# Recurrent layers: the scan's end states copied by ScalarE instead of VectorE, and the norm's power issued in two halves, one before and one after the next step's adding transfer

## The chip, the cores and the metric

The kernel runs on one core of a Trainium2 chip. The metric is the device time of one execution in microseconds (us). The engines are named as in the profile: PE is the matrix engine (PEld its weight loads), DVE is VectorE, ACT is ScalarE, POOL is GpSimd, SP issues plain transfers. Each engine works through its own instructions in the order in which the program wrote them[...].

## The reference

Four blocks follow each other on x of 4 batches x 512 positions x 512 channels, all in 32-bit floats: a cross attention (layer 0), two RWKV layers (layers 1 and 2), and a perceiver layer with an MLP (layer 3). The change touches layers 1 and 2 alone. In each of these, after the projections r, k, v, g and the decay w, a recurrence runs over the positions for every head (32 heads of 16 channels), and its output is normalised per head:

```python
def step(s, inp):
    k_l, v_l, w_l, r_l = inp
    a = k_l[..., :, None] * v_l[..., None, :]
    out = jnp.einsum('bhs,bhst->bht', r_l, faaaa * a + s)
    return a + w_l[..., None] * s, out
_, outs = jax.lax.scan(step, s0, seq)
gm = jnp.mean(y, axis=-1, keepdims=True)
gv = jnp.mean((y - gm) ** 2, axis=-1, keepdims=True)
y = ((y - gm) * jax.lax.rsqrt(gv + EPS)).reshape(B, L, C) * gn_w + gn_b
x = x + y * g @ Wo.T
```

The factor `rsqrt(gv + EPS)` is the power that the change cuts in two. The state s that one half of a sequence leaves to the other is what the copies carry. Around this stand a layer norm and the mixing of neighbouring positions before the recurrence, and a channel block (norm, two gates, three products) after it.

## The kernel before, in words

**Units and steps.** A unit is one layer, one batch and one half of the 512 positions: 16 units, numbered 0 to 15 here. Even units are first halves, odd units second halves, which start from the state that the even unit before them left. A unit has eight scan steps, 0 to 7 here. They are global steps g = 8 * unit + step, and one loop runs over g. At each g it emits, in this order: `summed(g - 1)` (four matmul groups on PE that sum the step before over the state), `begun(g + 1)`, `scan(g)`, at every fourth step `repeated` (PE writes the v rows of the coming four steps into the PSUM tile `vr`), and then whatever the generators have put down for this step in four phases, EARLY, SOON, MID and LATE. In the MID phase of steps 0 and 4, `taken` (L894) adds the sums `py` of the four steps before to `y`.

**What a step does.** `begun(g + 1)` (L833 to L844) has DVE write two products of k and v, one into the tile `kv` (two buffers, used in turn) and one into the tile `A` (a single buffer), and the state into the first column of `kv` (the copy at L839). Then POOL issues a transfer that adds `A` onto `kv` in SBUF (`added`, L584), and ACT spreads the decay into the tile `W` (L844). `scan(g)` (L862) runs the recurrence on DVE over `kv`; two more DVE products (`ry`, L867) follow, for PE. In even units a small DVE copy at L864 stands between the scan and the products; it saves the last column of `kv` as the state `S`. So one step's adding transfer has to land before DVE may write `A` for the following step, and before its own `kv` is scanned.

**What else runs in the steps.** Three generators per unit are laid over the steps by hand: each `yield` names the step, counted from the unit's own first step, and the phase in which the generator goes on. `mixes(q)` prepares unit q in the twelve or so steps before it (norm, projections, decay), `outputs(q)` normalises unit q from its step 9, that is step 1 of the following unit, and `channels(q)` does the channel block from step 19, that is step 3 of the unit after that. In a given unit, work of three other units is thus interleaved. After unit 15 the steps go on without scans until the last generators are done; this stretch, about 2,290 to 2,412 us, is called the drain here. Then layer 3 begins.

**The power.** `outputs` forms the variance on PE, adds the epsilon on DVE (L927, step 10, LATE), raises 128x64 values to the power -0.5 on POOL (L929, step 11, EARLY), and spreads the result over `rp` with four ACT copies (L933, step 12, LATE). PE multiplies `rp` out at step 13 (`pbc`), ACT copies it (L938), and DVE scales y with it (L940). On POOL's queue the power is followed, still in step 11, by the two small norm instructions of `channels` (L79 and L552) and by two adding transfers of the channel block (`x<-xr`, L584), and then, in step 12, by the adding transfer of `begun(13)`. Counted in the unit whose scan is running, the power stands in step 3 and that transfer belongs to step 5's `kv`.

**Three more names.** `td` (L735) and `o_w` (L744, L750) are ACT's work on the decay of the next unit, in the LATE phase of step 2 and the EARLY phase of step 3; they wait for PE. `o_g` (L717) is DVE's gating of g around step 6, which frees the PSUM tiles that PE's transposes `ptn` (L572) want next.

Of the kernel before, what the change touches and what calls it, by code (L numbers as in the profile page):

```python
# [11 lines left out]
ALU = mybir.AluOpType  # L12
# [18 lines left out]
def tile_xattn_rwkv_perceiver(ctx: ExitStack, tc: tile.TileContext, t: dict, out: bass.AP):  # L31
    nc = tc.nc
# [7 lines left out]
    mhalf = const.tile([P, TS // 4], F32, name="mhalf")  # L40
# [30 lines left out]
    def mm(ps, pairs):  # L71
        for i, (lhsT, rhs) in enumerate(pairs):
            nc.tensor.matmul(ps, lhsT, rhs, start=(i == 0), stop=(i == len(pairs) - 1))  # L73
# [22 lines left out]
    def psum_tile(shape, name):  # L96
        pool, tag = psum["p"]
        return pool.tile(shape, F32, tag=tag, name=name)
# [356 lines left out]
    def recurrent(lp, ep):  # L455
# [5 lines left out]
        TP = TS // 2  # L461
        EARLY, SOON, MID, LATE = range(4)
# [67 lines left out]
        def flat(a):  # L530
            return a.rearrange("p a l -> p (a l)")
# [314 lines left out]
        def place(g):  # L846
            q, j = divmod(g, G)
            return q, j // NI, j % NI

        def quarters(kv):  # L850
            return kv.rearrange("p (q f) l -> p q f l", f=2)

        def states(q):
            return st[q]["S"].rearrange("p i (q e f) -> p i e q f", e=2, f=2)

        def scan(g):

            q, e, i = place(g)
            d = st[q]
            kv = kvs.pop(g)  # L860

            nc.vector.tensor_tensor_scan(flat(kv), flat(W[g % 2]), flat(kv), 0.0, ALU.mult, ALU.add)  # L862
            if units[q][2] == 0:
                nc.vector.tensor_copy(states(q)[:, i, e], quarters(kv)[:, :, :, TP])  # L864
            for h in range(2):
                y = ys[g, h] = mp.tile([P, 4, 2, TP], F32, tag="ry", name="ry", bufs=4)
                nc.vector.tensor_tensor(  # L867
                    y,
                    kv[:, 4 * h : 4 * h + 4, None, :TP].to_broadcast([P, 4, 2, TP]),
                    d["r"][:, i].rearrange("p (o m) -> p o m", o=2)[:, None].to_broadcast([P, 4, 2, TP]),  # L870
                    ALU.mult,
                )
# [23 lines left out]
        def outputs(q):  # L896

            li, b, hf = units[q]
            n = f"L{li}_"
            c, d = small[li], st[q]  # L900
            y = d["y"]
            NQ = TS // 4
            full = [P, NI, TS]
            pm = psum_tile([P, TS], "pmean")
            mm(pm, [(gmean, y[:, i, :]) for i in range(NI)])
            mean = sp.tile([P, TS], F32, tag="mean", name="mean", bufs=1)
            nc.scalar.copy(mean, pm)
            yield 9, LATE
            nc.vector.tensor_tensor(y, y, mean[:, None, :].to_broadcast(full), ALU.subtract)
            yield 10, EARLY  # L910
            sq = mp.tile(full, F32, tag="cx", name="sq", bufs=BUFS["cx"])
            nc.scalar.activation(sq, y, AF.Square)
            yield 10, SOON
            var = psum_tile([P, NQ], "var")
            for i in range(NI):
                for a in range(4):
                    nc.tensor.matmul(
                        var[32 * a : 32 * a + 32],
                        gm32,
                        sq[:, i, NQ * a : NQ * a + NQ],  # L920
                        start=(i == 0),
                        stop=(i == NI - 1),
                        tile_position=(0, 32 * a),
                    )
            yield 10, LATE
            rstd = sp.tile([P, NQ], F32, tag="gn_rs", name="gn_rs")
            nc.vector.tensor_scalar(rstd, var, 1.0, 1e-5, ALU.mult, ALU.add)  # L927
            yield 11, EARLY
            nc.gpsimd.tensor_tensor(rstd, rstd, mhalf[:, :NQ], ALU.pow)  # L929
            yield 12, LATE  # L930
            for a in range(4):
                rs = slice(32 * a, 32 * a + 32)
                nc.scalar.copy(rp[rs, NQ * a : NQ * a + NQ], rstd[rs])  # L933
            yield 13, EARLY
            pm = psum_tile([P, TS], "pbc")
            mm(pm, [(gself, rp)])
            bc = sp.tile([P, TS], F32, tag="mean", name="bc", bufs=1)
            nc.scalar.copy(bc, pm)  # L938
            yield 13, LATE
            nc.vector.tensor_tensor(y, y, bc[:, None, :].to_broadcast(full), ALU.mult)  # L940
            yield 14, EARLY

            yg = mp.tile(full, F32, tag="cx", name="yg", bufs=BUFS["cx"])
            for i in range(NI):
                nc.scalar.activation(
                    yg[:, i].rearrange("p (m o) -> p o m", o=2),
                    y[:, i].rearrange("p (o m) -> p o m", o=2),
                    AF.Identity,
                    bias=c["gn"][:, i, 1:2],
                    scale=c["gn"][:, i, 0:1],  # L950
                )
            nc.gpsimd.tensor_tensor(yg, yg, d["g"], ALU.mult)
            yield 15, MID
            wo = wpool.tile([P, NI, C], F32, tag="w", name=n + "wo")
            for a in range(4):
                nc.sync.dma_start(
                    wo[32 * a : 32 * a + 32], t[n + "Wo"].rearrange("(h a i) n -> a h i n", a=4, i=NI)[a]
                )
            pms = []
            for lt in range(NT):  # L960
                pm = psum_tile([P, C], "pm")
                mm(pm, [(yg[:, i, lt * P : (lt + 1) * P], wo[:, i, :]) for i in range(NI)])
                pms.append(pm)
            yield 15, LATE
            for lt in range(NT):
                x = xn[b][hf * NT + lt]
                nc.vector.tensor_tensor(x, pms[lt], x, ALU.add)
# [74 lines left out]
        steps = {}  # L1042
# [6 lines left out]
        for q in range(len(units)):  # L1049
            if q > 0:  # L1050
                follow(q, (-13 if q == 1 else -11, LATE), mixes(q))
            follow(q, (9, EARLY), outputs(q))
            follow(q, (19, LATE), channels(q))
        end = G * len(units)
        with (
            tc.tile_pool(name="rm", bufs=2) as mp,
            tc.tile_pool(name="rs", bufs=2) as sp,
            tc.tile_pool(name="rpv", bufs=1, space=PSUM) as pvr,
            tc.tile_pool(name="rpy", bufs=1, space=PSUM) as pyp,
            tc.tile_pool(name="rpp", bufs=3, space=PSUM) as pp,  # L1060
        ):
            psum["p"] = pp, "p"


            W = [mp.tile([P, 8, TP + 1], F32, tag=f"W{i}", name=f"W{i}", bufs=1) for i in range(2)]
            A = mp.tile([P, 8, TP + 1], F32, tag="A", name="A", bufs=1)
            for z in (*W, A):
                nc.gpsimd.memset(z[:, :, 0:1], 0.0)
            for g in range(at[0], end + 28):
                if 0 < g <= end:  # L1070
                    summed(g - 1)
                if -1 <= g < end - 1:
                    begun(g + 1)
                if 0 <= g < end:
                    scan(g)
                if 0 < g < end - 2 and g % NI == NI - 2:
                    repeated(*place(g + 2)[:2])
                for ph in (EARLY, SOON, MID, LATE):
                    for q, gen in steps.pop((g, ph), ()):
                        at = next(gen, None)  # L1080
                        if at:
                            follow(q, at, gen)
                    if ph == MID and 0 < g <= end and g % NI == 0:
                        taken(g - 1)
# [325 lines left out]
    with (  # L1410
        tc.manual_schedule(engines={E.PE, E.DVE, E.Activation, E.Pool}),
        tc.tile_pool(name="rl", bufs=1) as lp,
        tc.tile_pool(name="rt", bufs=2) as ep,
    ):
        ahead = recurrent(lp, ep)
        layer0(ahead, ep)
        for _ in ahead:
            pass
# [66 lines left out]
```

## Time and profile before

| what | value |
|---|---|
| time, median of 3 runs | 3794.02 us (3792.13 to 3795.58) |
| the profiled execution's own time | 3798.02 us |
| its span | 3796.2 us |
| granted PE clock, mean | 0.966 |
| scans of the 16 units | about 778 to 2,290 us |
| POOL power L929 (128x64) | 16, 11.65 us each |
| DVE copy of the state L864 | 64, 0.88 us each |
| DVE copy of the state L839 | 128, 0.17 us in the middle |
| DVE products L867 | 256, 1.40 us each |
| DVE waiting for an adding transfer before A L833 | 87.8 us, 38 times |

In the profile's lines a group reads: line, engine, operation, output<-inputs, size, count, then busy time, mean ns of one, and idle time of the engine before them with what ended it. In the timeline a line gives start, duration, engine, line, operation, and in brackets how long the engine had been idle and who released it; instructions of one line that follow each other are merged into one row with a count. Where an engine waits for several things, the row names the one that came last.

### The profile page before, as it was taken

What the parts mean: (1) busy time and instruction counts of PE and PEld (TensorE: products, weight loads), DVE (VectorE), ACT (ScalarE), POOL (GpSimd) and SP (SyncE); (2) the same over time, 40 slices, a digit from 0 to 9 for tenths busy, and PEclk for the clock granted to TensorE, in tenths of its full rate; (3) what the DMA queues carried; (4) which work ended last, traced back from release to release, by engine and by line L of the source; (5) the groups of instructions that cost most, each with busy time, mean ns of one, the idle gap of its engine ahead of it and who ended that gap; (6) DMA issues with size and microseconds to landing.
All of it is one profiled execution on the core that took longest, in us unless ns stands there. A gap on an engine that the chain in (4) does not pass through costs nothing.

```text
span 3796.2 us, 52369 instructions
## 1 busy us (share of the span) xinstructions
PE 3570.5 (94%) x20544; PEld 1900.4 (50%) x20544; DVE 2759.9 (73%) x4665; ACT 1668.2 (44%) x2486; POOL 1771.0 (47%) x834
## 2 busy tenths in 40 slices
PE   9999999988899999999999977799999999999989
PEld 3333333455565666655655544444455445544446
DVE  6777777689988888888888882177866766667531
ACT  4777675533444444444444432133334434434421
POOL 4777876524544444444444443045533433344330
PEclk9999999989999999999999988899999999999999
DMA  4000000156676777777777764400022122121223
GB/s 151 24 12 23 12 9 20 40 141 141 146 171 165 170 188 177 170 173 179 163 171 167 169 156 111 111 28 19 15 76 83 56 70 95 56 73 34 95 95 122
DMA packets 188805, 386.66 MB, mean 102 GB/s; under 512 B 18128, under 2 KB 44880, under 8 KB 186512
## 3 DMA queue, kind: packets, MB, share of 16 engines
q1 hardware_dynamic: 150256, 251.72, 20.9%
q0 software_dynamic: 38304, 131.61, 18.7%
q8 instruction: 162, 2.65, 0.3%
q14 instruction: 83, 0.68, 0.1%
HBM read 247.50 MB, written 4.19 MB: 66 GB/s over the span
## 4 chain that ended last, share of the span: by engine, by line
PE 71%; DVE 13%; DMA 6%; issue 4%; POOL 3%; ACT 2%; SPq 0%; DVEq 0%; POOLq 0%; ACTq 0%
PE pm L73 9%; PE ph L73 6%; PE pv L73 6%; PE po L73 6%; DMA kv<-A 5%; PE psc L242 5%; PE pst L279 4%; PE pst L1175 4%; PE psc L1175 4%; PE pr L73 3%; PE pk L73 3%; PE po L304 3%; PE po L1241 3%; DVE ry L867 3%; DVE kv L862 2%
## 5 line engine op out<-in xcount | busy, mean ns | idle before, releaser
L1236 POOL TENSOR_TENSOR acc<-acc,aT 128x2048 f32<-128x2048 f32 x96 | 436.2, 4544 | 337.5 <-ACT aT L1231 220.0
L292 POOL TENSOR_TENSOR aT<-aT,nmT 128x1536 f32<-128x1536 f32 x124 | 428.7, 3461 | 205.5 <-ACT aT L290 182.2
L254 DVE CUSTOM_DVE_ANT_0 sc<-psc,nm 128x512 f32<-128x512 f32 x512 | 354.1, 692 | 147.2 <-PE psc L242 89.5
L1220 DVE TENSOR_TENSOR aT<-pst,mb 128x512 f32<-128x512 f32 x512 | 317.7, 683 | 166.0 <-PE pst L1175 166.0
L867 DVE TENSOR_TENSOR ry<-kv,o_r 128x1024 f32<-128x1024 f32 x256 | 347.4, 1398 | 3.5
L584 POOL DMA_DIRECT2D kv<-A x127 | 118.8, 936 | 381.4 <-DVE kv L839 378.3
L862 DVE TENSOR_TENSOR_SCAN kv<-W,kv 128x1032 f32<-128x1032 f32 x128 | 296.3, 2315 | 0.2 <-DMA kv<-A 0.2
L290 ACT COPY aT<-pst 128x512 f32<-128x512 f32 x372 | 196.5, 595 | 177.9 <-PE pst L279 177.4
L298 ACT ACTIVATE aT<-aT 128x2048 f32<-128x2048 f32 x128 | 246.7, 1929 | 5.4 <-POOL aT L292 4.6
L73 PE MATMUL ph<-nT,l_m 128*128 128x256 f32 x1024 | 238.1, 388 | 0.0
L73 PE MATMUL po<-l_m,hT 128*128 128x512 f32 x512 | 233.1, 602 | 0.0
L73 PEld LDWEIGHTS ph<-nT,l_m 128*128 128x128 f32 x1024 | 193.6, 193 | 64.1 <-issue 24.8
L833 DVE TENSOR_TENSOR A<-vr,o_k 128x1024 f32<-128x1024 f32 x128 | 155.7, 1217 | 87.9 <-DMA kv<-A 87.8
L279 PE MATMUL pst<-q,km 32*128 32x512 f32 x1024 | 206.5, 640 | 9.4 <-DVE mxs L254 5.8
L1234 POOL TENSOR_TENSOR acc<-aT 128x2048 f32<-128x2048 f32 x16 | 72.4, 4527 | 303.2 <-ACT aT L1229 303.2
L1189 DVE CUSTOM_DVE_ANT_0 sc<-psc,zeros,mx 128x512 f32<-128x512 f32 x256 | 176.6, 746 | 51.2 <-PE psc L1175 49.0
L1231 ACT ACTIVATE aT<-aT 128x2048 f32<-128x2048 f32 x64 | 122.3, 1911 | 191.8 <-DVE aT L1220 191.6
L1229 ACT ACTIVATE aT<-aT,mc 128x2048 f32<-128x2048 f32 x64 | 128.1, 2002 | 165.1 <-DVE aT L1220 158.9
L242 PE MATMUL psc<-km,q 32*128 32x512 f32 x1024 | 198.5, 651 | 0.8 <-ACT q L223 0.8
L929 POOL TENSOR_TENSOR gn_rs<-gn_rs,mhalf 128x64 f32<-128x64 f32 x16 | 186.4, 11648 | 23.1 <-DVE gn_rs L927 23.1
L881 PE MATMUL py<-ry,k 128*32 128x512 f32 x1024 | 159.6, 637 | 39.1 <-DVE ry L867 27.6
L1189 DVE CUSTOM_DVE_ANT_0 sc<-psc,nm 128x512 f32<-128x512 f32 x256 | 161.1, 686 | 39.2 <-PE psc L1175 39.2
(265 smaller groups left out, 7153.3 us busy)
## 6 DMA issues: line engine op xcount, KB each, us to landing
l_m<-in_L_W SPq DMA_DIRECT2D x64, 1024.0 KB, 5.1
kv<-A POOLq DMA_DIRECT2D x127, 516.0 KB, 7.4
L_wk<-in_L_Wk SPq DMA_DIRECT2D x16, 1024.0 KB, 8.0
L_wr<-in_L_Wr SPq DMA_DIRECT2D x16, 1024.0 KB, 7.7
L_wv<-in_L_Wv SPq DMA_DIRECT2D x16, 1024.0 KB, 5.9
L_wg<-in_L_Wg SPq DMA_DIRECT2D x16, 1024.0 KB, 8.0
L_wo<-in_L_Wo SPq DMA_DIRECT2D x64, 256.0 KB, 7.6
L_fk<-in_L_fWk SPq DMA_DIRECT2D x16, 1024.0 KB, 7.8
```

The costliest lines, as they stand in the source:

```text
L73: nc.tensor.matmul(ps, lhsT, rhs, start=(i == 0), stop=(i == len(pairs) - 1))
L242: nc.tensor.matmul(psc, d["q"][g][rs, lt * P : (lt + 1) * P], d["km"][rs, a, :], start=True, stop=True, tile_position=(32 * r, 0),)
L254: nc.vector.tensor_tensor_reduce(sc, ps[r], d["nm"][lt], 1.0, -3.0e38, ALU.add, ALU.max, mxs[:, a, lt, c : c + 1])
L279: nc.tensor.matmul(pst, d["km"][rs, a, s * P : (s + 1) * P], d["q2", a][rs, :], start=True, stop=True, tile_position=(32 * r, 0),)
L292: nc.gpsimd.tensor_tensor(w[:, n:, :], w[:, n:, :], nmT[:, None, :].to_broadcast([P, NR - n, L]), ALU.add)
L298: nc.scalar.activation(w, w, AF.Exp)
L862: nc.vector.tensor_tensor_scan(flat(kv), flat(W[g % 2]), flat(kv), 0.0, ALU.mult, ALU.add)
L867: nc.vector.tensor_tensor(y, kv[:, 4 * h : 4 * h + 4, None, :TP].to_broadcast([P, 4, 2, TP]), d["r"][:, i].rearrange("p (o m) -> p o m", o ...
L1175: nc.tensor.matmul(psc, lhsT[rs], rhs[rs], start=True, stop=True, tile_position=(32 * r, 0))
L1189: nc.vector.tensor_tensor_reduce(sc, ps[r], d["nm"][a], 1.0, mx[:, 0, lt, r : r + 1] if a else 3.0e38, ALU.add, ALU.min, mx[:, a, lt, r : ...
L1220: nc.vector.tensor_tensor(w[:, r, :], ps[r], d["mb"][:, r, :], ALU.subtract)
L1236: nc.gpsimd.tensor_tensor(d["acc", m], d["acc", m], w, ALU.add)
```

## The change

The copy of the end state leaves DVE's place behind the scan. It is put down as a small generator `kept` that runs in the SOON phase of the same step, behind that step's EARLY work, as an ACT copy. The power on 128x64 is replaced by two on 128x32: the first stands where the whole one stood (step 11, EARLY), the second in the EARLY phase of step 12, behind the adding transfer that `begun(13)` issues at the start of step 12. The step and phase in which the ACT copies to `rp` are emitted stay.

```diff
@@ -853,6 +853,10 @@
+        def kept(dst, src):
+            nc.scalar.copy(dst, src)
+            yield from ()
+
         def scan(g):
@@ -861,7 +865,7 @@
             nc.vector.tensor_tensor_scan(flat(kv), flat(W[g % 2]), flat(kv), 0.0, ALU.mult, ALU.add)
             if units[q][2] == 0:
-                nc.vector.tensor_copy(states(q)[:, i, e], quarters(kv)[:, :, :, TP])
+                steps.setdefault((g, SOON), []).append((q, kept(states(q)[:, i, e], quarters(kv)[:, :, :, TP])))
@@ -926,7 +930,9 @@
             nc.vector.tensor_scalar(rstd, var, 1.0, 1e-5, ALU.mult, ALU.add)
             yield 11, EARLY
-            nc.gpsimd.tensor_tensor(rstd, rstd, mhalf[:, :NQ], ALU.pow)
+            nc.gpsimd.tensor_tensor(rstd[:, : NQ // 2], rstd[:, : NQ // 2], mhalf[:, : NQ // 2], ALU.pow)
+            yield 12, EARLY
+            nc.gpsimd.tensor_tensor(rstd[:, NQ // 2 :], rstd[:, NQ // 2 :], mhalf[:, : NQ // 2], ALU.pow)
             yield 12, LATE
             for a in range(4):
```

## The prediction

> **What bounds the kernel now.** I read the page's busy times and its chain first, then a table of stretches, then the timelines of PE, POOL, DVE and ACT through the scans.
>
> ```profile
> PE 3570.5 (94%) x20544; PEld 1900.4 (50%) x20544; DVE 2759.9 (73%) x4665; ACT 1668.2 (44%) x2486; POOL 1771.0 (47%) x834
> PE 71%; DVE 13%; DMA 6%; issue 4%; POOL 3%; ACT 2%; SPq 0%; DVEq 0%; POOLq 0%; ACTq 0%
> 1200.00:1600.00 400.00, 376.44 (x2535) 242.32 (x2536) 355.00 (x371) 180.94 (x360) 188.86 (x123) 0.99 0.75 176
> ```
>
> The third line is a stretch of four units: PE 376 of 400 us, DVE 355, ACT 181, POOL 189, clock 0.99, the DMA engines 75% busy. In the scans PE is the bound and a unit takes 95 to 100 us; what can be won is PE's idle time, 5 to 7 us a unit. Time taken off DVE, ACT or POOL counts only where PE stops for it. So I listed every stop of PE and asked which of them leads back to the power. Around the power of unit 7, POOL first:
>
> ```profile
> 1465.00 0.85 POOL L584 DMA_DIRECT2D kv<-A  x1 [1.79 <-DVE kv L839]
> 1465.56 11.72 POOL L929 TENSOR_TENSOR gn_rs<-gn_rs,mhalf 128x64 f32<-128x64 f32 x1
> 1477.26 0.69 POOL L79 TENSOR_TENSOR rs_cx<-rs_cx,mhalf 128x2 f32<-128x2 f32 x1
> 1479.62 1.81 POOL L584 DMA_DIRECT2D x<-xr  x2
> 1480.79 1.53 POOL L584 DMA_DIRECT2D kv<-A  x1
> ```
>
> and DVE and PE beside it:
>
> ```profile
> 1472.23 0.16 DVE L78 TENSOR_SCALAR rs_cx<-ln_mv 128x2 f32<-128x2 f32 x1
> 1477.28 0.20 DVE L839 COPY kv<-S 128x8 f32<-128x8 f32 x1
> 1484.99 0.69 DVE L894 TENSOR_TENSOR y<-py,y 128x512 f32<-128x512 f32 x1 [2.84 <-PE py L881]
> 1490.96 1.22 DVE L833 TENSOR_TENSOR A<-vr,o_k 128x1024 f32<-128x1024 f32 x1 [3.01 <-DMA kv<-A]
> 1502.97 1.14 PE L814 MATMUL vr<-o_v,vsel 32*128 32x512 f32 x8 [0.45 <-DVE A L833]
> 1516.56 1.12 PE L572 MATMUL ptn<-ident,z 128*128 128x128 f32 x4 [2.92 <-DVE o_g L717]
> ```
>
> DVE has all that the transfer needs at 1477.5, but POOL is behind the power, two small norm instructions and two other adding transfers, and issues it at 1480.79. It lands at 1490.93, DVE writes the next A 3.01 late, the transfer after that lands late too, and PE stops for DVE's A before vr (0.45) and for o_g before ptn (2.92). Over units 1 to 13 the stops before vr that follow a power are 1.98, 3.83, 0.26, 1.50, 1.24, 0.45, 2.50, 2.44, 0.19 and 2.57 (units 1, 2, 3, 4, 5, 7, 9, 10, 11, 13), 16.96 us in all. Before ptn, six units (3, 4, 5, 7, 11, 12) stop for 2.8 to 3.0.
>
> **The power in halves.** A 128x32 power is not in the trace. From the rows 11.72 (64 columns) and 0.69 (2 columns) it is 0.178 a column, so 0.69 + 30 x 0.178 = 6.0; below, half of 11.72 is 5.9; above, the whole 11.72, which 0.69 for two columns excludes. I take 6.0. In unit 7 the first half ends at 1471.6; the norm's 0.69 waits for DVE until 1472.4, its second instruction (0.2 where nothing holds it, 1.6 at most) and the two transfers (1.8) are out by 1475.3 to 1476.7. The transfer is issued when DVE allows it, at 1477.28 + 0.46 (the distance in the step before, 1464.54 to 1465.00) = 1477.7: 3.1 us earlier. The same sum gives 4.6 in unit 1, about 6 in 2 and 13, 4.5 in 5 and 9. The second half lies at 1478.3 to 1484.3. Behind it on POOL is the adding transfer of mix_g, which DVE frees only at 1487, and ACT's copies to rp come at 1492: 3 and 8 us of cover. Without that cover the next transfer would be late by the part that sticks out, 6.0 at most.
>
> What PE gets: 16.96 less the 0.16 by which unit 2's stop (3.83) exceeds the wait before A that can vanish (3.67), so 16.8. The 2.9 before ptn falls only to what units have in which DVE is earlier: stops before ptn plus the following one before py are 1.7, 2.0, 1.2, 0.8 and 1.3 in units 6, 8, 9, 10, 13, mean 1.4. So 1.5 in each of six units, 9.0.
>
> A rule speaks against this part. The Trainium skill ("SBUF — State Buffer", Who interferes with whom) says that a DVE instruction with two SBUF inputs is blocked by a POOL instruction that reads SBUF, for all of its length. Then the second half would hold step 4's ry from 1479.8 to 1484.3; it would end at 1486.6, y (L894) would follow 1.6 later than now, and 15 units would pay up to 24 us. But ry at 1466.95 took 2.36 for its pair in the middle of the whole power, as without it. For the power the row decides: nothing.
>
> **The copies.** Rows and rule agree on the 128x1024 products of POOL:
>
> ```profile
> 1371.33 0.17 DVE L864 COPY S<-kv 128x8 f32<-128x8 f32 x1
> 1407.24 3.26 POOL L772 TENSOR_TENSOR ruk<-ruk,o_k 128x1024 f32<-128x1024 f32 x1
> 1408.37 2.17 DVE L864 COPY S<-kv 128x8 f32<-128x8 f32 x1
> 1435.31 4.33 DVE L867 TENSOR_TENSOR ry<-kv,o_r 128x1024 f32<-128x1024 f32 x2
> ```
>
> The copy is 0.17 (0.08 until the next begins) or, in 23 of 64, about 2.1, held to the end of a POOL product. Read alone, that is 23 x 2.1 = 48 us to win on DVE. But ry also has two SBUF inputs, and in odd units, which have no copy, the ry at the same places is held instead (4.33 for a pair of 2.35). The hold goes to ry; DVE keeps 64 x 0.09 = 6 us, off PE's path: nothing. On ACT a 128x8 copy isn't in the trace; 128x4 and 32x64 take 0.20 and 0.24: 0.2 each, 13 us, under ACT's 56% idle.
>
> The new wait costs more. The next-but-one kv uses the same buffer, so DVE may not write it before ACT has copied, and ACT copies only behind its EARLY work. In step 3 that is o_w, which waits for PE (unit 6):
>
> ```profile
> 1376.75 1.22 DVE L833 TENSOR_TENSOR kv<-vr,o_k 128x1024 f32<-128x1024 f32 x1
> 1379.35 1.06 ACT L750 ACTIVATE o_w<-o_w 128x1024 f32<-128x1024 f32 x1
> 1389.26 0.69 DVE L894 TENSOR_TENSOR y<-py,y 128x512 f32<-128x512 f32 x1 [2.35 <-PE py L881]
> ```
>
> The kv product moves from 1376.75 to 1380.7, A from 1380.93 to 1381.8, and the transfer goes out at 1383.6: 1.9 earlier than now, not 3.0. In units 4, 8, 10 and 12 the same sum leaves 2.0, 1.3, 2.5 and 1.4, still about what their stops need. Everything queued on DVE behind (A, the scan, ry) is late by 1.0, 1.1, 3.1, 1.8 and 4.1 in units 4, 6, 8, 10, 12, against 2.42, 2.35, 4.51, 3.18 and 5.51 that DVE waits for py before y anyway: covered. In step 1 the copy is behind mix_r and costs DVE 0.7, in step 7 ACT waits 0.9 for the scan, with xr behind it; both vanish in later waits. I add nothing.
>
> **The end.** In unit 15's scan the power of unit 14 (2250.90) holds the transfer until 2265.90; DVE has it ready at 2260.4, and all that follows waits for it: 5.5 less, I take 5.4. In the drain it turns round:
>
> ```profile
> 2330.34 0.16 DVE L78 TENSOR_SCALAR rs_cx<-ln_mv 128x2 f32<-128x2 f32 x1
> 2332.76 1.52 ACT L561 ACTIVATE z<-x,ln_mv,rs_cx 128x512 f32<-128x512 f32 x2
> 2332.93 1.83 POOL L584 DMA_DIRECT2D x<-xr  x2 [0.28 <-issue]
> 2341.90 1.22 PE L73 MATMUL pm<-L_wo,yg 128*128 128x512 f32 x1 [5.80 <-POOL yg L952]
> ```
>
> The whole power started at 2321.13 while POOL had nothing else. The second half stands behind the norm that waits for DVE until 2330.5 and behind two transfers, so it runs from about 2333.4 to 2339.2; ACT's rp ends 1.0 later, and z, queued behind it, starts at 2340.0 instead of 2332.76. The chain goes on through yg to PE without slack: +7.2.
>
> **Sum.** -16.8 - 9.0 - 5.4 + 7.2 = -24.0. The profiled execution: span 3796.2 and 1.8 around it, 3798.0, so 3774.0. The median shown is 4.0 under that execution, so I forecast 3770.
>
> **Rivals.**
> - *The transfers land no earlier.* They share DMA engines that are 70 to 75% busy, and took 7.4 in the middle but 12.3 in unit 9. If half of the body's 25.8 goes there or into the next stop: -11, 3783. For it: the landing times vary. Against: the queue only gets the same transfers sooner. Chance 0.2.
> - *More than summed.* Stops before ptn vanish whole (six x 1.4), and unit 14's stops (2.78 before py) fall: -35, 3759. Chance 0.13.
> - *Nothing comes of it* (within 8 us): POOL's lateness is replaced by the kv write behind o_w, in odd units by DMA. Chance 0.1.
> - *Slower: DVE's kv write behind ACT's o_w.* At the whole 4.0 in six even units: +24, less the odd units' 9.2 before vr, with the end's +1.8: +17, 3811. It decides once DVE's wait before y (L894) is shorter than the delay; at 2.35 to 5.51 against 1.0 to 4.1 it isn't, but an earlier PE shortens it. Chance 0.17.
>
> **How the numbers follow.** The likeliest case has 0.4: 3770, its own range 3764 to 3777. Leaving 0.08 below and 0.12 above, the range is 3757 to 3802. What a measurement of this kernel can tell from no change is about 0.2%, 8 us. Faster: 0.4 + 0.2 x 0.8 + 0.13 = 0.69; same: 0.1 + 0.2 x 0.2 = 0.14; slower 0.17.
>
> **What would show it.** Two POOL powers of about 6 us, with kv<-A between them; waits before A of 3 to 6 us in step 5 down to 0 to 2; PE's stops before vr gone and those before ptn at 0.5 to 1; ry held where S<-kv was; the kv product of step 4 in even units waiting on ACT; the wait on the last power longer. I am wrong if the landing times grow by what the issue gains, if PE waits for ry or py in even units where it now doesn't, or if a half takes much more than 6 us.

## The result, and the profile after

The changed kernel takes 3758.76 us (median of 4 runs, 3754.79 to 3761.84), beside 3794.80 for the kernel before (4 runs, 3792.13 to 3797.16): a ratio of 0.9896, 95% interval 0.9879 to 0.9913. The forecast of 3770 was right in direction and 11 us too cautious; 0.9896 of the 3794.02 that the forecast started from is 3754.6, just below the low end of its range. The profiled execution of the changed kernel took 3754.79 us with a span of 3753.1, 43.1 us less than the span before. That pair overstates the gain: the execution before was some 3 us above its median, the one after was the fastest of its four.

First the page's busy row of the changed kernel, then its stretch from 1200 to 1600 us. A stretch's line gives its length, then busy time and count of PE, PE's weight loads, DVE, ACT and POOL, then the granted clock (1.00 is full speed), the DMA share and GB/s:

```profile
PE 3551.1 (95%) x20544; PEld 1888.2 (50%) x20544; DVE 2730.6 (73%) x4601; ACT 1675.2 (45%) x2550; POOL 1743.5 (46%) x850
1200.00:1600.00 400.00, 384.29 (x2691) 244.35 (x2690) 346.99 (x356) 191.53 (x396) 183.77 (x130) 1.00 0.76 178
```

PE is busy for 384 of 400 us instead of 376, and its clock is at 1.00. But over the whole program PE's busy time also fell, by 19.4 us (3570.5 to 3551.1), with the same 20544 matmuls. Waiting less can't do that. It is the first sign of what the forecast lacked.

POOL around the power in unit 7's scan:

```profile
1452.18 0.85 POOL L584 DMA_DIRECT2D kv<-A  x1 [1.79 <-DVE kv L839]
1452.74 6.60 POOL L933 TENSOR_TENSOR gn_rs<-gn_rs,mhalf 128x32 f32<-128x32 f32 x1
1459.65 0.69 POOL L79 TENSOR_TENSOR rs_cx<-rs_cx,mhalf 128x2 f32<-128x2 f32 x1 [0.30 <-DVE rs_cx L78]
1460.64 1.82 POOL L584 DMA_DIRECT2D x<-xr  x2
1463.89 0.86 POOL L584 DMA_DIRECT2D kv<-A  x1 [1.43 <-DVE kv L839]
1464.45 6.60 POOL L935 TENSOR_TENSOR gn_rs<-gn_rs,mhalf 128x32 f32<-128x32 f32 x1
```

DVE and PE beside it:

```profile
1462.29 1.23 DVE L833 TENSOR_TENSOR A<-vr,o_k 128x1024 f32<-128x1024 f32 x1 [1.59 <-DMA kv<-A]
1465.90 2.36 DVE L871 TENSOR_TENSOR ry<-kv,o_r 128x1024 f32<-128x1024 f32 x2
1472.17 0.69 DVE L898 TENSOR_TENSOR y<-py,y 128x512 f32<-128x512 f32 x1 [3.91 <-PE py L885]
1475.05 1.22 DVE L833 TENSOR_TENSOR A<-vr,o_k 128x1024 f32<-128x1024 f32 x1
1489.63 1.14 PE L814 MATMUL vr<-o_v,vsel 32*128 32x512 f32 x8
1500.89 0.66 PE L572 MATMUL ptn<-ident,z 128*128 128x128 f32 x4 [0.58 <-DVE o_g L717]
```

POOL now waits for DVE before the transfer (1.43), not DVE for POOL. The transfer is issued 11.2 us after the power's start instead of 15.2. A is written at 1475.05 with no wait, where it waited 3.01. PE's stop before vr is gone, the one before ptn is 0.58 instead of 2.92. The ry at 1465.90 takes 2.36 for its pair in the middle of the second half.

**Where the 43.1 us are.** Cut at the starts of the powers, in the profiled executions:

| stretch | before | after | difference | forecast |
|---|---|---|---|---|
| 700 us to the power in unit 3's scan | 372.9 | 371.3 | -1.6 | -5.65 (the stops of units 1 and 2) |
| from there to the power in unit 14's scan ("units 3 to 13" below) | 1087.0 | 1051.2 | -35.8 | -20.15 |
| from there to the power of unit 15 | 161.3 | 149.1 | -12.2 | -5.4 |
| from there to the end | 1475.1 | 1481.5 | +6.5 | +7.2 |

The stops of PE in units 3 to 13, listed one by one from the timeline, fell from 61.7 to 40.8 us: before vr by 11.15 (to nothing), before ptn by 14.0, and before py they grew by 4.25. That is 20.9 against a forecast of 20.15. The other 15 of the 35.8 us are busy time. The same stretch of the kernel before,

```profile
1072.88:2159.84 1086.96, 1024.86 (x6888) 650.81 (x6887) 941.32 (x980) 486.24 (x968) 508.37 (x332) 0.98 0.74 172
```

and after:

```profile
1071.27:2122.47 1051.20, 1009.58 (x6889) 642.38 (x6888) 915.11 (x937) 490.25 (x1011) 483.59 (x342) 1.00 0.77 178
```

The matmuls are the same (6888 and 6889), but PE is busy for 15.3 us less, at a granted clock of 1.00 instead of 0.98. The trace records the clock in pieces of 3.4 us or multiples of it. In this stretch 47.8 us were at half clock before (14 such pieces of 3.4 us), and 3.4 us after (1 piece). In the kernel before it looks like this in the timeline of PE,

```profile
1796.33 1.06 PE L881 MATMUL py<-ry,k 128*32 128x512 f32 x8
1799.84 2.09 PE L814 MATMUL vr<-o_v,vsel 32*128 32x512 f32 x8 [2.44 <-DVE A L833]
```

and in the stretch of 4 us that follows:

```profile
1800.00:1804.00 4.00, 4.00 (x20) 2.14 (x24) 3.97 (x2) 0.99 (x3) 3.84 (x2) 0.50 0.90 221
```

After the stop of 2.44 the eight vr matmuls take 2.09 us instead of the 1.14 of other units: the clock column stands at 0.50.

**Which stops bring half clock.** Not every stop does. The prediction's ptn at 1516.56 took 1.12 us behind a stop of 2.92. In unit 5 of the same kernel it took 0.66 behind a stop of 2.90:

```profile
1323.07 0.66 PE L572 MATMUL ptn<-ident,z 128*128 128x128 f32 x4 [2.90 <-DVE o_g L717]
```

What differs is where the stop lies. In each trace all pieces at half clock begin on one grid of 3.413 us (to within 2 ns), which cuts the time into windows. The stop of 2.92 puts 2.43 us of idle PE into one window; the stop of 2.90 is shared by two, 1.35 and 1.55. In units 3 to 13 of the fourteen profiles (both kernels and the experiments below), all 26 windows with 1.98 us or more of idle PE were followed by half clock, 6 of the 9 with 1.81 to 1.94, and none of the 22 with 1.35 to 1.76. The other pieces are of two kinds. 27 follow a window with 2.3 to 2.7 us of the `pmm` matmuls of `mixes` (32*128 in their rows) around a stop of 0.5 to 0.6: all 25 windows with 2.40 us or more of them, 2 of the 8 with 2.31 to 2.39, and none of the 606 with 1 to 2.3. Such matmuls stand in every unit, but in some only does a window of the grid take in so many. Six continue a piece. Of the 14 pieces before, 8 follow a stop, 1 continues such a piece, and 5 follow `pmm`. The one after the change follows `pmm`.

### The profile page after: what moved, and what is told of

Same layout as the page of the kernel before. It is cut to its first block, busy times and chain, and to the rows that moved or that the text cites. A ratio compares the mean times of both kernels' runs of the same rounds, so it can differ in the third digit from the quotient of the medians.

```text
span 3753.1 us, 52451 instructions
## 1 busy us (share of the span) xinstructions
PE 3551.1 (95%) x20544; PEld 1888.2 (50%) x20544; DVE 2730.6 (73%) x4601; ACT 1675.2 (45%) x2550; POOL 1743.5 (46%) x850
## 5 line engine op out<-in xcount | busy, mean ns | idle before, releaser
L871 DVE TENSOR_TENSOR ry<-kv,o_r 128x1024 f32<-128x1024 f32 x256 | 398.5, 1598 | 7.2 <-DVE kv L866 0.5
L885 PE MATMUL py<-ry,k 128*32 128x512 f32 x1024 | 162.0, 624 | 38.4 <-DVE ry L871 25.5
L1181 PE MATMUL pst<-q,kT 32*128 32x512 f32 x1024 | 182.2, 648 | 0.1
L1181 PE MATMUL psc<-kT,q 32*128 32x512 f32 x1024 | 171.4, 648 | 11.5 <-DVE aT L1226 11.5
```

The costliest lines, as they stand in the source:

```text
L871: nc.vector.tensor_tensor(y, kv[:, 4 * h : 4 * h + 4, None, :TP].to_broadcast([P, 4, 2, TP]), d["r"][:, i].rearrange("p (o m) -> p o m", o ...
L1181: nc.tensor.matmul(psc, lhsT[rs], rhs[rs], start=True, stop=True, tile_position=(32 * r, 0))
```

## Experiments

All kernels were timed against runs of the kernel before on the same chip in the same session; its median was 3790.1, 3789.1, 3792.7, 3791.6 and 3793.3 in the five sessions. "Units 3 to 13" is the second stretch of the table above, "half clock" the time in it at half the granted clock. Lengths, stops and half clock are of one profiled execution each, the times are medians. An edit is shown against the changed kernel, where nothing else is said.

### The copies alone

```diff
-            nc.gpsimd.tensor_tensor(rstd[:, : NQ // 2], rstd[:, : NQ // 2], mhalf[:, : NQ // 2], ALU.pow)
-            yield 12, EARLY
-            nc.gpsimd.tensor_tensor(rstd[:, NQ // 2 :], rstd[:, NQ // 2 :], mhalf[:, : NQ // 2], ALU.pow)
+            nc.gpsimd.tensor_tensor(rstd, rstd, mhalf[:, :NQ], ALU.pow)
```

> The change with the power left whole: only the copies of the states move to ScalarE. Theory (the halves carry the gain; the hold of a DVE instruction behind a POOL product passes from the copy to ry): 3788 to 3802 us, within 0.2% of before; the stops of PE before vr and ptn as before (about 31 us in units 3 to 13), 10 to 16 half-clock windows between the powers of units 3 and 13, and ry's busy time up by about 50 us while the copy's 50 leave DVE. Rival (the freed DVE time carries a part of the gain): 3770 to 3785 us, with fewer stops. Rival (DVE's kv product behind ACT costs): 3803 to 3815 us, with PE waiting for py or vr in even units.

Measured: 3777.46 us (22 runs), ratio 0.9966 (0.9957 to 0.9976), some 12.7 us faster. Units 3 to 13 took 1069.9 us with 20.5 us at half clock. The theory missed; the time is the first rival's. The hold did pass to ry as forecast (between 760 and 2200 us DVE's copy took 56.3 us before and is gone, and ry's busy time rose from 320.4 to 372.7), so the copies still give DVE nothing worth having. Something else brings 12.7 us.

### The halves alone

```diff
-                steps.setdefault((g, SOON), []).append((q, kept(states(q)[:, i, e], quarters(kv)[:, :, :, TP])))
+                nc.vector.tensor_copy(states(q)[:, i, e], quarters(kv)[:, :, :, TP])
```

> The change with the copies left on DVE: only the power is in halves. Theory (the halves carry the gain): 3755 to 3765 us, the stops of PE in units 3 to 13 at about 41 us instead of 62, and at most 3 half-clock windows there instead of 14. Rival (the copies carry a part): 3768 to 3782 us. Rival (the wait of the kv product behind ACT costs something in the full change): below 3753 us, with no wait of 3.5 us before kv.

Measured: 3762.52 us (6 runs), ratio 0.9927 (0.9909 to 0.9946). Units 3 to 13 took 1051.3 us with stops of 41.2 and 3.4 us at half clock: the full change's 1051.2, 40.8 and 3.4. In the body the halves alone do all of it. The gains of the two parts don't add: whichever comes second finds little left.

### Both halves ahead of the transfer

```diff
             nc.gpsimd.tensor_tensor(rstd[:, : NQ // 2], rstd[:, : NQ // 2], mhalf[:, : NQ // 2], ALU.pow)
-            yield 12, EARLY
             nc.gpsimd.tensor_tensor(rstd[:, NQ // 2 :], rstd[:, NQ // 2 :], mhalf[:, : NQ // 2], ALU.pow)
```

> The change with both halves of the power in a row ahead of the adding transfer, copies on ScalarE. Theory (it is the place of the transfer between them that counts): two halves of 6.5 us are 13.0 against 11.7 for the whole, so the transfer goes out 1.3 us later than before, and the time is 3794 to 3806 us, with 12 or more half-clock windows in units 3 to 13. Rival (shorter instructions on POOL hold others less, wherever they stand): 3757 to 3775 us.

Measured: 3784.10 us (22 runs), ratio 0.9982 (0.9974 to 0.9991). It lies between the two expectations, for two reasons. It has the copies on ScalarE, so it is to be compared with 3777.46, not with 3790: it is 6.6 us slower than that. And the halves took 6.60 and 5.42 us, 12.0 together, not 13. The place of the transfer is what counts.

### The last power whole

```diff
-            nc.gpsimd.tensor_tensor(rstd[:, : NQ // 2], rstd[:, : NQ // 2], mhalf[:, : NQ // 2], ALU.pow)
-            yield 12, EARLY
-            nc.gpsimd.tensor_tensor(rstd[:, NQ // 2 :], rstd[:, NQ // 2 :], mhalf[:, : NQ // 2], ALU.pow)
+            if q == len(units) - 1:
+                nc.gpsimd.tensor_tensor(rstd, rstd, mhalf[:, :NQ], ALU.pow)
+            else:
+                nc.gpsimd.tensor_tensor(rstd[:, : NQ // 2], rstd[:, : NQ // 2], mhalf[:, : NQ // 2], ALU.pow)
+                yield 12, EARLY
+                nc.gpsimd.tensor_tensor(rstd[:, NQ // 2 :], rstd[:, NQ // 2 :], mhalf[:, : NQ // 2], ALU.pow)
```

> The full change, but the last unit's power (unit 15's, in the drain) stays whole, as before. Theory (in the drain the second half stands behind the norm that waits for DVE, and the chain through rp, yg and the output product has no slack): 6 to 7 us less than the full change, 3750 to 3754 us, PE's stop before pbc in the drain back from 12.4 to about 5. Rival (the drain is bound by the other chain, and what rp wins is lost again before ptn or pq): 3757 to 3762 us.

Measured: 3754.77 us (6 runs), ratio 0.9905 (0.9886 to 0.9925). The full change, run again below in another session, has 3760.22, so the last power in halves costs some 5.5 us; a pair from one session, with the copies on DVE in one of them, gives 5.4 (3760.22 and 3754.86). The drain of the full change, and then of this kernel:

```profile
2283.44 6.11 POOL L935 TENSOR_TENSOR gn_rs<-gn_rs,mhalf 128x32 f32<-128x32 f32 x1
2290.64 1.22 PE L73 MATMUL pbc<-rp,gsel 128*128 128x256 f32 x2 [12.41 <-ACT rp L939]
```

```profile
2292.22 1.22 PE L73 MATMUL pbc<-rp,gsel 128*128 128x256 f32 x2 [4.97 <-ACT rp L942]
```

The second half ran from 2283.44 behind the norm and its transfers, and PE's stop grew from 4.97 to 12.41.

### Which copy brings the gain

In the full change DVE's kv product of step 4 waits for ScalarE's copy of step 3, as forecast (3.5 to 3.9 us in even units). Two kernels with the power whole split the eight copies. One has only step 3's on ScalarE (shown against "The copies alone"):

```diff
-            if units[q][2] == 0:
+            if units[q][2] == 0 and g % G == 3:
                 steps.setdefault((g, SOON), []).append((q, kept(states(q)[:, i, e], quarters(kv)[:, :, :, TP])))
+            elif units[q][2] == 0:
+                nc.vector.tensor_copy(states(q)[:, i, e], quarters(kv)[:, :, :, TP])
```

> Power whole. Of a unit's eight copies of the states only that of step 3 is on ScalarE (behind o_w), the other seven stay on DVE. Theory W (the new wait itself brings the gain of the copies: it holds DVE's kv product, A and scan in even units for about 1.2 us, so that POOL's two small norm instructions behind the power run ahead of the scan, 0.69 us instead of 1.6 to 2.6, and the adding transfer goes out some 4 us sooner): most of the 12.7 us that all copies gave, 3774 to 3783 us, and even units' scans of 95 us. Theory D (DVE is freed of copies that POOL held for 2.1 us each): one copy of eight gives a small part, 3786 to 3792 us.

The other has `!= 3` in place of `== 3`.

> The mirror image: power whole, seven of a unit's eight copies on ScalarE, that of step 3 on DVE, so that no kv product waits for ScalarE behind o_w. Theory W: the gain goes, 3785 to 3793 us, with even units at 99 us. Theory D: most of the gain stays, 3774 to 3782 us.

Measured: 3779.93 us (14 runs), ratio 0.9971 (0.9959 to 0.9983), for the one copy; 3789.53 us (14 runs), ratio 1.0000 (0.9987 to 1.0012), for the other seven. So the gain of the copies comes from the one copy for which DVE has to wait: 9 of the 12.7 us with it, none without it. In unit 10 of the kernel before, POOL's norm instruction, the transfer behind it, and DVE's next A:

```profile
1771.91 2.30 DVE L862 TENSOR_TENSOR_SCAN kv<-W,kv 128x1032 f32<-128x1032 f32 x1
1772.14 2.56 POOL L79 TENSOR_TENSOR rs_cx<-rs_cx,mhalf 128x2 f32<-128x2 f32 x1
1776.72 1.53 POOL L584 DMA_DIRECT2D kv<-A  x1
1788.52 1.23 DVE L833 TENSOR_TENSOR A<-vr,o_k 128x1024 f32<-128x1024 f32 x1 [5.69 <-DMA kv<-A]
```

and with the one copy on ScalarE:

```profile
1761.81 1.23 DVE L833 TENSOR_TENSOR kv<-vr,o_k 128x1024 f32<-128x1024 f32 x1 [3.87 <-ACT S L857]
1762.81 0.69 POOL L79 TENSOR_TENSOR rs_cx<-rs_cx,mhalf 128x2 f32<-128x2 f32 x1
1764.15 2.30 DVE L866 TENSOR_TENSOR_SCAN kv<-W,kv 128x1032 f32<-128x1032 f32 x1
1764.97 1.53 POOL L584 DMA_DIRECT2D kv<-A  x1
1773.42 1.21 DVE L833 TENSOR_TENSOR A<-vr,o_k 128x1024 f32<-128x1024 f32 x1
```

Without the wait, DVE's scan begins just before the power ends, and POOL's 0.69 us instruction takes 2.56 beside it. With the wait the scan begins later, POOL slips through in 0.69, and the transfer goes out 13.9 us after the power's start instead of 16.3. A then waits for nothing. The new wait that I booked as a cost was the gain.

### The full change again, and the halves with the last power whole and the copies on DVE

> The full change once more, beside the others. Theory (the end stretch and the first units vary from one execution to the next, the units 3 to 13 don't): 3755 to 3762 us, units 3 to 13 within 1 us of 1051.2, 0 or 1 half-clock windows there; the stretch from the power of unit 14 to that of unit 15 longer than in the first profile (62.9) by up to 7.

Measured: 3760.22 us (6 runs), ratio 0.9916 (0.9899 to 0.9932); units 3 to 13 in 1052.9, the end stretch 149.0 again, so it didn't grow.

The second kernel joins the edits of "The halves alone" and "The last power whole".

> Power in halves in units 0 to 14, whole in unit 15, all copies on DVE as before. Theory (with the power in halves the copies are worth nothing, and the last second half costs 6): 3751 to 3758 us, within 0.1% of the same with the copies on ScalarE. Rival (the copies keep a part of their gain): 3760 to 3768 us.

Measured: 3754.86 us (5 runs), ratio 0.9902 (0.9885 to 0.9920). With the copies on ScalarE it was 3754.77 (0.9905, in another session). Where the power is in halves, the copies are worth nothing. These two are the fastest kernels of the study.

### A delay on DVE by other means

Against the kernel before:

```diff
-            for half, dst in ((seconds, kv), (firsts, A)):
+            again = ((firsts, A),) if g % G == 5 else ()
+            for half, dst in ((seconds, kv), (firsts, A), *again):
```

> The kernel before, power whole and copies on DVE, with one useless instruction a unit added on DVE: the product A of step 4 is written twice, 1.2 us. Theory W (holding DVE's scan back lets POOL's norm instructions run ahead of it): faster than before although work was added, 3774 to 3785 us, the scans of even units at 95 to 97 us and the norm's power instruction at 0.69 there. Rival (DVE's time is what counts): 1.2 us more in each of 15 units, 3790 to 3808 us.

Measured: 3796.52 us (10 runs), ratio 1.0011 (0.9998 to 1.0024): the theory missed on the time. In the profiled execution, the fastest of the ten at 3789.47, it holds scan by scan: in 4 of the 11 the delayed scan began 12.7 us or more after the power's start, and POOL had its two instructions done by then or all but done, in 0.69 and 0.2 us; those four transfers went out at 13.9 to 14.2, A waited for nothing and the units took 95.1 to 97.0 us. In the seven others the delay put the scan at 10.3 to 11.9, on top of POOL's instructions, the transfer went out at 15.1 to 17.3, and the units took 97.6 to 99.8. A delay helps only if it carries the scan past POOL; the wait on ScalarE always did, 1.2 us of added work didn't.

### The power moved, not halved

Against the kernel before:

```diff
+            if q < len(units) - 1:
+                yield 12, EARLY
             nc.gpsimd.tensor_tensor(rstd, rstd, mhalf[:, :NQ], ALU.pow)
```

> Copies on DVE as before, and the power not halved at all: in units 0 to 14 the whole power is moved to step 12, behind the adding transfer, in unit 15 it stays. Theory (what counts is that the transfer goes out ahead; the power needs to be there only for ScalarE's rp, 14 us after that transfer in the full change): the whole power would end 5.1 us later than the second half, before rp, and put mix_g's transfer 2.7 us later and the next adding transfer 1.5 us later, both under waits: 3751 to 3758 us, units 3 to 13 at 1050 to 1053. Rival (the halving is needed: mix_g's or the next adding transfer lands late): stops before vr or ptn come back, 3765 to 3785 us.

Measured: 3765.35 us (5 runs), ratio 0.9923 (0.9909 to 0.9937). The theory missed on the time: this is some 8 us slower than the halves with the last one whole (0.9902, in another session). Units 3 to 13 took 1054.9, nearly as forecast. The rest is lost where ScalarE's rp comes soon after: in two of the first units (4.17 and 5.11) and in unit 15's scan (6.40) PE stops before pbc.

```profile
1006.57 1.22 PE L73 MATMUL pbc<-rp,gsel 128*128 128x256 f32 x2 [5.11 <-ACT rp L935]
2243.02 1.22 PE L73 MATMUL pbc<-rp,gsel 128*128 128x256 f32 x2 [6.40 <-ACT rp L935]
```

In the kernel with halves these stops are 0.74 and 1.28. So the power is best started early and finished late, which is what the halves do.

### A cut at 48 and 16 columns

```diff
-            nc.gpsimd.tensor_tensor(rstd[:, : NQ // 2], rstd[:, : NQ // 2], mhalf[:, : NQ // 2], ALU.pow)
+            nc.gpsimd.tensor_tensor(rstd[:, : 48], rstd[:, : 48], mhalf[:, : 48], ALU.pow)
             yield 12, EARLY
-            nc.gpsimd.tensor_tensor(rstd[:, NQ // 2 :], rstd[:, NQ // 2 :], mhalf[:, : NQ // 2], ALU.pow)
+            nc.gpsimd.tensor_tensor(rstd[:, 48 :], rstd[:, 48 :], mhalf[:, : 16], ALU.pow)
```

> The full change with the power cut at 48 and 16 columns instead of 32 and 32. The first part then takes about 9.1 us and the norm's two instructions end some 2.5 us later than with halves. Theory T (a threshold: an adding transfer issued no later than 14.2 us after the power's start lands before DVE wants it, at 22.3; later ones land at 23 to 28): the transfer still goes out at 11 to 13.5, so units 3 to 13 take 1050 to 1054 us with at most 2 half-clock windows, and the time is 3753 to 3762 us. Theory P (every microsecond by which the transfer goes out sooner counts): half of the gain goes, 3770 to 3780 us.

Measured: 3761.00 us (6 runs), ratio 0.9917 (0.9903 to 0.9932), units 3 to 13 in 1051.3: the same as with halves, though the first part took 9.19 us. Theory T, a threshold, holds. When the transfer goes out, and when A can be written, both counted from the power's start, with the length up to the next power, in us:

| scan of unit | before: issue, A, length | copies alone | full change |
|---|---|---|---|
| 3 | 14.9, 24.3, 99.8 | 15.1, 24.7, 99.9 | 9.5, 22.3, 96.0 |
| 4 | 15.3, 26.8, 98.7 | 13.6, 21.7, 94.8 | 13.0, 21.7, 94.7 |
| 5 | 15.5, 27.0, 98.6 | 15.2, 26.7, 100.2 | 11.2, 22.3, 95.8 |
| 6 | 15.6, 23.9, 95.6 | 13.6, 22.1, 95.2 | 13.3, 21.9, 95.0 |
| 7 | 15.2, 25.4, 99.5 | 15.2, 26.1, 99.6 | 11.2, 22.3, 95.8 |
| 8 | 15.0, 24.3, 96.0 | 13.6, 22.1, 95.2 | 13.3, 21.9, 95.0 |
| 9 | 16.0, 28.2, 99.4 | 15.8, 27.7, 99.3 | 11.4, 22.3, 95.8 |
| 10 | 16.3, 28.1, 101.5 | 13.6, 21.9, 95.0 | 13.3, 21.9, 95.0 |
| 11 | 15.3, 25.5, 99.4 | 14.7, 23.0, 95.8 | 10.4, 22.3, 97.3 |
| 12 | 15.1, 24.6, 99.1 | 13.6, 21.9, 95.0 | 13.4, 22.1, 95.2 |
| 13 | 15.8, 28.3, 99.5 | 16.3, 28.5, 100.1 | 11.0, 22.3, 95.8 |

Up to about 14.2 us A comes at 21.7 to 22.4, set by DVE's own order, and nothing is won by an earlier issue; the same holds for all 97 such scans of twelve profiles. From 14.6 on A waits, and each microsecond of lateness costs about 3 in the kernel before, about 2.5 over all 45 late scans, with misses of some 2 us. Why the landing grows so fast there wasn't tried.

### Stops put in on purpose

```diff
-            for a in range(4):
+            for a in 3 * list(range(4)) if q % 2 else 2 * list(range(4)):
                 rs = slice(32 * a, 32 * a + 32)
                 nc.scalar.copy(rp[rs, NQ * a : NQ * a + NQ], rstd[rs])
```

> The full change with stops of PE put in on purpose: ScalarE's four copies to rp, for which PE waits 0.74 us before pbc, are made twice in even-numbered units' norms (a stop of about 1.74 us) and three times in odd ones (about 2.74, the length of the stops of the kernel before). Theory C (a stop of 2.5 to 2.9 us lowers the clock for the matmuls behind it, one of 1.7 doesn't): in units 3 to 13 at least 4 half-clock windows instead of 1 or 2, behind the longer stops, PE's busy time there 1013 us or more instead of 1010 to 1012, and the time 8 to 30 us over the full change. Rival (the clock goes its own way): at most 2 windows, busy time 1010 to 1012, and the time longer only by what is left of the stops, 0 to 17 us.

Measured: 3796.06 us (20 runs), ratio 1.0010 (1.0000 to 1.0019), 36 us over the full change's 3760.22: six more than I had allowed. In units 3 to 13 the stops grew by 17.8 us, to 58.6, and the stretch by 31.6, to 1082.8; half clock rose from 3.4 to 34.1 us. Its line of that stretch:

```profile
1070.14:2152.98 1082.84, 1023.33 (x6888) 648.32 (x6887) 913.29 (x937) 506.20 (x1075) 477.82 (x342) 0.98 0.75 173
```

PE is busy 13.7 us more than after the change (1009.58), with the same matmuls; one of the places, in PE's timeline,

```profile
1591.45 1.22 PE L73 MATMUL pbc<-rp,gsel 128*128 128x256 f32 x2 [2.91 <-ACT rp L939]
```

and as a stretch:

```profile
1591.00:1595.00 4.00, 3.55 (x9) 2.94 (x10) 1.32 (x5) 3.20 (x7) 0.91 (x2) 0.57 0.61 226
```

So stops bring half clock with them, and Theory C holds in that. Its detail doesn't: three of the ten pieces at half clock stand behind stops of 1.84 us, two behind stops of 2.91, and five follow `pmm`. The full change has one piece of the last kind, and two when it ran again: how many there are varies in one and the same kernel, so not all of the 13.7 us can be put down to the stops. A fit over the fourteen profiles gives an estimate: PE's busy time in units 3 to 13 grows by 1.1 us for a piece that follows a stop or continues one, and by 1.7 for one behind `pmm`, with misses of up to 1.5. The four pieces behind `pmm` that this kernel and the kernel before have more than the full change would then be some 7 us in each.

All profiled kernels, units 3 to 13, in us (rest: length less stops):

| kernel | length | PE's stops | half clock | rest |
|---|---|---|---|---|
| before | 1087.0 | 61.7 | 47.8 | 1025.3 |
| stops put in | 1082.8 | 58.6 | 34.1 | 1024.2 |
| A written twice | 1075.2 | 58.0 | 23.9 | 1017.3 |
| halves joined | 1073.2 | 54.9 | 23.9 | 1018.4 |
| all copies but one | 1072.5 | 55.0 | 27.3 | 1017.5 |
| copies alone | 1069.9 | 52.5 | 20.5 | 1017.4 |
| one copy | 1066.6 | 51.0 | 17.1 | 1015.6 |
| power moved | 1054.9 | 44.0 | 3.4 | 1010.9 |
| halves alone | 1051.3 | 41.2 | 3.4 | 1010.1 |
| 48 and 16 | 1051.3 | 40.8 | 3.4 | 1010.5 |
| full change | 1051.2 | 40.8 | 3.4 | 1010.4 |

Against the full change, every microsecond of stops costs 1.4 to 1.8 of time in the kernels of the upper seven rows. The two at 1.7 to 1.8, the kernel before and the stops put in, are those with five pieces behind `pmm`. The two that have one, as the full change has, stand at 1.4 (A written twice) and 1.5 (all copies but one), so some 1.4 is the price of the stops themselves.

## Why the prediction was right or wrong

- **What bounds the kernel** was right: PE does, and the gain is PE's.
- **The power in halves, its durations.** 6.0 us a half was too low: 6.36 to 6.60 in most units. The row of 0.69 for two columns, from which it was worked out, stands right behind another power, and a half right behind another took 5.42, about 1.2 less. It cost nothing, because a first part of up to 9.2 us is early enough. The cover of the second half was there in units 3 to 13. How much of it is needed is shown by the whole power behind the transfer, which is some 8 us worse.
- **What PE gets.** The list of stops, units 3 to 13, was sized well: -20.9 against -20.15, with the stops before vr gone and those before ptn plus py at 1.4. **The step that failed is the price of a stop.** The sum took a stop off at its own length and put the clock at nothing. In fact PE's matmuls behind a stop run partly at half clock, and 15 us of PE's busy time went with the 21 us of stops. At the factor of 35.8 / 20.9 = 1.71 the forecast's 20.15 would have been 34.5. Some 7 of the 15 us (an estimate, see "Stops put in on purpose") belong to the pieces behind `pmm`, of which the profiled execution before happened to have four more; at 1.4 the 20.15 would have been 28. The profile before held the sign for it: a granted clock of 0.99 in a stretch that I read as full speed, vr at 2.09 us beside 1.14, and ptn at 1.12 in the prediction's own lines beside 0.66 in unit 5. Units 1 and 2 gave 1.6 instead of 5.65; their stops before vr fell from 3.83 to 2.52 in unit 2, but one of 2.91 before ptn came up there.
- **The rule against it.** The row decided rightly: ry took 2.36 a pair in the middle of the second half, all 60 single products that lie inside a half took 1.22 to 1.27, and none of the 24 us came.
- **The copies.** Nothing, in the full change: right, as 3754.86 and 3754.77 show. The hold passed to ry as said. But with the power whole the same copies are worth 12.7 us, through the wait that the forecast entered as a cost: it lets POOL run ahead of DVE's scan. In the full change this is hidden, since the halves have already put POOL ahead.
- **The new wait.** It came as said (kv waits 3.5 to 3.9 in step 4 of even units), and DVE's wait before y covers it.
- **The end.** +7.2 in the drain: 6.5 in the profile, and 5.4 to 5.5 in the timed runs without it. Unit 15's scan gave 12.2 in the profile against 5.4; with other kernels that have the same halves there it gave 6.2 to 12.3, so this part is not settled.
- **The rivals.** The time is that of "more than summed" (3759), by another cause, so that agreement is luck: the stops before ptn did not vanish whole. "Nothing comes of it" is refuted by the time. "The transfers land no earlier" is refuted: A's waits in step 5 are gone in all eleven scans. The slower rival is refuted too: with the power whole, its wait makes the kernel faster.

The sum, mended for units 3 to 13 alone, would have been -38 with the factor of 1.71 and -32 with 1.4; the pair of profiles gave -43.1, the timed pairs -36.0 and -28.9. The second pair has 27 runs of the kernel before instead of 4, and its ratio of 0.9916 would have put the time at 3762, inside the forecast's range. So the forecast gain was too small by 5 to 12 us.

## What to carry to other kernels

A stop of PE in a stretch that is otherwise full costs more than its length: look at the granted clock and at the same matmul's duration behind a stop, and price the stops here at some 1.4 times their sum. A single stop can cost its length alone or more, by how it lies to the windows of the clock; stops well below 1.8 us, away from `pmm`, brought no half clock. What is worth moving is what carries a transfer across the point from which it lands late (here 14.2 us); two edits that cross the same point don't add, so each is to be run alone and both together. A long instruction on a queue that also issues transfers is well cut where the next transfer stands, but not in the stretch where nothing comes behind it to be saved.

## What the runs showed of the hardware

- PE's clock fell to half for 3.4 us at a time behind stops as short as 1.84 us, when enough of the stop lay in one window of a grid of 3.413 us (26 of 26 windows with 1.98 us or more of idle PE, 6 of 9 with 1.81 to 1.94, none of 22 with 1.35 to 1.76). It fell too behind all 25 windows that held 2.40 us or more of `pmm` and a stop of 0.5 to 0.6, and behind none of 606 with 1 to 2.3 us of it. The Trainium skill ("TensorE: Matmul & The Clock Gate", Part 1: The HAM clock gate) speaks of an idle window of about 3.4 us that runs freely, without regard to the kernel; the grid here fits that. Its rule there is to have no gaps over some 3.4 us. Every stop before vr, pbc or ptn in units 3 to 13 was shorter than that (2.96 at most), and the measured pieces decide: by that rule none of the 14 pieces would be there, and the forecast's price would be right. The same part tells of a kernel in which short idles between groups of matmuls made the clock swing, without saying how short.
- POOL's power on 128x2 takes 0.69 us, and up to 2.73 when DVE's scan runs beside it; on 128x32, 128x48 and 128x64 it takes 6.60, 9.19 and 11.72, that is 0.16 us a column and 1.5 at the start (128x16 varied, 3.3 to 4.9). About 1.2 of the start is missing in a half right behind another (5.42) and in the drain (10.57 for 128x64); on what this depends is open.
- A useful delay: DVE held for 3.9 us by a wait in every other unit made the kernel 9 us faster (3789.1 to 3779.9), since another engine's short instruction got in ahead.
